# Requests for broadcast rows moved to later cycles, inverse rows made by exponentials, and a reordered last block

## The chip, the cores and the metric

The kernel runs on one core of a Trainium2 chip. The metric is the device time of one execution in microseconds (us). A core has five engines that each work through their own queue of instructions: TensorE (PE in the profile, its weight loads apart as PEld), VectorE (DVE), ScalarE (ACT), GpSimd (POOL) and SyncE (SP). SP and POOL ask for most of the transfers between the chip's main memory (DRAM) and the on-chip memory. Matrix products are written to PSUM[...].

## The reference

Two layers over 4096 nodes with 512 features, each followed by a residual and a layernorm. Layer 0 is graph attention with 8 heads of 64 features and a dense 0/1 adjacency of 4096 x 4096; its cost is the sums over all pairs of nodes.

```python
feats = jnp.einsum('nf,hfo->hno', X, W)
s_self = jnp.einsum('hno,ho->hn', feats, a_self)
s_neigh = jnp.einsum('hno,ho->hn', feats, a_neigh)
dense = s_self[:, :, None] + s_neigh[:, None, :]
dense = jnp.where(dense > 0, dense, ALPHA * dense)      # ALPHA = 0.2
dense = dense * A[None, :, :]
attn = jax.nn.softmax(dense, axis=-1)
out = jnp.einsum('hij,hjo->hio', attn, feats) + b[:, None, :]
...
x = _layernorm(x + relu(out of all heads side by side))
...
# layer 1: attention inside 32 graphs of 128 nodes, with query, key, value products,
# the adjacency added to the scores twice; then again residual and layernorm
```

## The kernel before, in words

The exponential of a leaky sum of two scores is the larger of two products of factors that belong to one node each, so a pair costs no exponential of its own. Setup computes for every node and head the factors exp(s), exp(0.2 s), exp(0.8 s) and exp(-0.2 s). For the receiving node (index i, along the free axis) they are needed as rows that are the same in all 128 partitions: row p = exp(0.8 s_i) and row u = exp(-0.2 s_i), and for some heads also U = 1/u. For the sending node (index j, along the partitions) they are columns: `d_all`, `e_all`, its bf16 parts `e_b`, and `c_all`, the reciprocal of one of them.

**Setup** runs over 8 blocks of four 128-node tiles. Per block: transposes of x, the feature products (L818), the scores, exponentials on ScalarE (L750, L751, L754), scaled features to DRAM (`f_d`, `g_d`), and the function `rows_of_exponentials`: two reciprocals (L780) on VectorE make U for the first and last pair of heads, four transposes (L786) turn the block's columns into 20 rows, ScalarE copies them (L793), POOL writes them to `pu_d` in DRAM. `parts_of_exponentials` makes `c_all` with two reciprocals per block (L762).

**The main part** is `main_pass(r)` for r = 0 to 3, one pair of heads each. A pass has 4 chunks (c) of 1024 receiving nodes, and a chunk goes over the 32 sending tiles j in cycles: eight tiles per cycle in passes 0 to 2, four in pass 3. For a tile j and each of the two heads

- VectorE makes q = max(p_row, d) times the adjacency tile (L1534),
- a mark of where the max took p_row is made by ScalarE (L1544) or, for every fourth tile's second head, by VectorE (L1539),
- TensorE adds q times g_s into `acc` (L1581), the adjacency tile times f_s into `accf` (L1558, four matmuls per tile), and the marks times e_b into `dens` (L1597).

A *folded* tile leaves out the L1558 products. VectorE makes its q with two operations instead of one (L1522 with the U row, L1525 with c_all), and TensorE adds q into `accf` instead of `acc`. In pass 0 the folded tiles are 10 and 18 in chunk 0 and 2, 10 and 18 in the others; in pass 3 a table gives them.

Within a cycle the order on TensorE is written out by hand: L1558 for all tiles of the cycle, transposes for the first half of the next cycle's adjacency (L617, pass 0 only), L1581 for all tiles, L1597, sums over the adjacency (L1479, pass 0), transposes for the other half. q has 8 buffers, so VectorE works up to four tiles ahead of L1581.

In pass 0 the adjacency arrives from DRAM as a_b: POOL asks for blocks of four tiles (L605, three buffers, each asked for ten tiles ahead at a fixed place of POOL's order), TensorE transposes them, ScalarE casts them to `at` (L628), and POOL writes each `at` tile to `at_d` for the later passes (L629). Passes 1 to 3 read `at_d`.

SP asks per chunk for the rows: p (two rows of 512 KB, L1434, two buffers each), u (two halves of 256 KB, L1440, one buffer), and U where tiles are folded (two of 512 KB, L1462, in the buffers `ck`); and per four tiles for f_s (512 KB, L1496) and g_s (256 KB, L1501), two buffers each. The p and u requests stand at the head of a chunk in the program; for chunks 0 and 1 of pass 0 they are kept in program order, otherwise a scheduler that plans all engines but TensorE may move them ahead as far as buffers allow.

At the end of a chunk VectorE combines the sums, (accf + S) * u_row (L1278), then adds acc (L1286); transposes and scaling follow in pieces during the next chunk.

**The last part** is layer 1, in 8 blocks of four 128-node rows; most of it runs between cycles of pass 3, the rest after it. For the last block `values(u)` makes a value product (L1186, four products of 512 columns, each two matmul records in the trace) and adds a bias on VectorE (L1194), and `rows_out` multiplies by the attention (L1200), adds the residual (L1202), and does the layernorm (L520, L521 on VectorE, L523, L524 on POOL, L528 on VectorE) and the output transfer. Before: values 2, values 3, then rows 2, rows 3.

Of the kernel before, what the change touches and what calls it, by code (L numbers as in the profile page):

```python
# [10 lines left out]
F32 = mybir.dt.float32  # L11
# [393 lines left out]
def adjacency_streamed_path(  # L405
# [58 lines left out]
    FOLDED = (0, PR - 1)  # L464
    FOLDS = {4: (1,), 5: (0, 1), 6: (0, 1, 2)}, {2: (1,), 4: (1,), 5: (0, 1), 6: (0, 1, 2)}
    HU = 2 * len(FOLDED)
    pu_d = dram.tile([2 * H + HU, N], F32, name="pu_d")
    at_d = dram.tile([NCH, NT, P, C], F32, name="at_d")
# [17 lines left out]
    for c in range(FC):  # L486
# [11 lines left out]
    nb_all = const.tile([P, NT, H], F32, name="nb_all")  # L498
    c_all = {
        r: (const if r else early).tile([P, NT, 2], F32, name="c_all") for r in FOLDED  # L500
    }
    below_0 = const.tile([P, 1], F32, name="below_0")
# [136 lines left out]
    with tc.tile_pool(name="setup1", bufs=1, side="right") as one, tc.tile_pool(  # L639
# [60 lines left out]
        for c in range(FC // 2):  # L700
            score_columns(c, False)
        powers = one.tile([P, 5, H], F32, name="powers")
        for i, v in enumerate((ALPHA, 1.0, ALPHA - 1.0, 1.0 - ALPHA, -ALPHA)):
            nc.vector.memset(powers[:, i, :], v)
# [32 lines left out]
        def exponentials(k, u, sc):  # L737

            j = 4 * k + u
            if u == 0:  # L740
                pu_js[k] = two.tile([P, 4, 2 * H + HU], F32, name="pu_j")
            st = small.tile([P, 5, H], F32, name="st")
            for lo, hi, w in ((0, 3, 1), (3, 5, 0)):
                ends_of_setup["DVE", u] = nc.vector.tensor_tensor(
                    st[:, lo:hi].rearrange("p k (q h) -> p k q h", q=2),
                    sc[:, None, :, :, w].to_broadcast([P, hi - lo, 2, H // 2]),
                    powers[:, lo:hi].rearrange("p k (q h) -> p k q h", q=2),
                    OP.mult,
                )
            nc.scalar.activation(e_all[:, j], st[:, 0:2], AF.Exp)  # L750
            nc.scalar.activation(  # L751
                pu_js[k][:, u, : 2 * H].rearrange("p (k h) -> p k h", k=2), st[:, 3:5], AF.Exp
            )
            nc.scalar.activation(d_all[:, j, :], st[:, 2], AF.Exp)  # L754

        def parts_of_exponentials(k):
            blk = slice(4 * k, 4 * k + 4)
            nc.vector.tensor_scalar_mul(
                nb_all[:, blk, :], d_all[:, blk, :], -BIG * (1.0 + 2.0**-23)
            )  # L760
            for r in FOLDED:
                nc.vector.reciprocal(  # L762
                    c_all[r][:, blk], e_all[:, blk, 1, 2 * r : 2 * r + 2]
                )
            eb = e_b[:, blk]
            for i in range(2):
                src = e_all[:, blk, i, :]
                rest = small.tile([P, 4, H], F32, name="rest")
                nc.vector.tensor_copy(eb[:, :, :, 3 * i], src)
                nc.vector.tensor_sub(rest, src, eb[:, :, :, 3 * i])  # L770
                nc.vector.tensor_copy(eb[:, :, :, 3 * i + 1], rest)
                nc.vector.tensor_sub(eb[:, :, :, 3 * i + 2], rest, eb[:, :, :, 3 * i + 1])
            nc.vector.tensor_copy(
                e_p[:, blk, :NE].rearrange("p j (m h) -> p j h m", h=H), eb[:, :, :, :3]
            )
            nc.vector.tensor_scalar_mul(eb[:, :, :, :3], eb[:, :, :, :3], -1.0)

        def rows_of_exponentials(k):
            for i, r in enumerate(FOLDED):
                nc.vector.reciprocal(  # L780
                    pu_js[k][:, :, 2 * H + 2 * i : 2 * H + 2 * i + 2],
                    pu_js[k][:, :, H + 2 * r : H + 2 * r + 2],
                )
            pr = pss.tile([2 * H + HU, 4, P], F32, name="ps_set")
            for u in range(4):
                nc.tensor.transpose(pr[:, u, :], pu_js[k][:, u], ident)  # L786
            if k < NB - 1:
                row = late.tile([2 * H + HU, 4 * P], F32, name="pu_row")
            else:
                row = hp_.tile([P, CT, FP], F32, name="hst")  # L790
                row = row.rearrange("p t n -> p (t n)")[: 2 * H + HU, : 4 * P]
            rows[k] = row
# [295 lines left out]
    def layer_1(blk, x1b, lp, lp1, lp2):  # L1088
# [93 lines left out]

        def values(u):
            pv = misc([P, F])
            for f in range(FC):
                nc.tensor.matmul(  # L1186
# [5 lines left out]
                )  # L1192
            vs[u] = lp.tile([P, F], F32, name="v_t")
            nc.vector.tensor_add(vs[u], pv, L1["bv"])  # L1194

# [26 lines left out]
        values(2)  # L1222
        values(3)
        yield
        if blk == NT // 4 - 1:
            rows_out((2,))
            rows_out((3,))
        else:
            rows_out((2, 3))
        yield  # L1230
# [193 lines left out]
    steps = [(r, c, j) for r in range(PR) for c in range(NCH) for j in range(NT)]  # L1424

    def main_pass(r, ae=None, wide=4):

        for c in range(NCH):
            p_row = []
            for h in range(2):  # L1430
                p_row.append(rowp.tile([P, C], F32, name=f"p_row{h}"))
                in_order(
                    r == 0 and c < 2,
                    nc.sync.dma_start(p_row[h], broadcast_rows(pu_d[2 * r + h, ts(c, C)], P, C)),  # L1434
                )
            u_row = urowp.tile([P, C], F32, name="u_row")
            for h in range(2):
                in_order(
                    r == 0 and c < 2,
                    nc.sync.dma_start(  # L1440
                        u_row[h * FH : (h + 1) * FH, :],
                        broadcast_rows(pu_d[H + 2 * r + h, ts(c, C)], FH, C),
                    ),
                )
            U_row = []

            def folded(j):

                if r == PR - 1:
                    return r in FOLDED and c > 0 and j % 4 in FOLDS[c > 1].get(j // 4, ())  # L1450
                return r in FOLDED and j % 8 == 2 and (0 if c else 8) < j < NT - 8

            def rows_for_folded():

                for h in range(2):
                    if r == PR - 1:
                        pool, shape, name = ((hp_, [P, CT, FP], "hst"), (pools.get("lp1"), [P, C], "U_row"))[h]
                    else:
# [4 lines left out]
                        U_row[h],  # L1463
                        broadcast_rows(pu_d[2 * H + 2 * FOLDED.index(r) + h, ts(c, C)], P, C),
                    )
# [24 lines left out]
            for j0 in range(0, NT, wide):  # L1490
# [3 lines left out]
                for k in range(j0 // 4, (j0 + wide) // 4):  # L1494
                    f_s[k] = fsp.tile([P, 4, 2, FP], F32R, name="f_s")
                    ins = nc.sync.dma_start(  # L1496
                        f_s[k].rearrange("p u s n -> p (u s n)").bitcast(F32), f_d[r, k]
                    )
# [4 lines left out]
                    )  # L1503
                    in_order(r == 0 and c == 0 and j0 < 16, ins)
                if at_step == 0:
                    cast_steps(0, 6, last_pair)
# [201 lines left out]
```

## Time and profile before

| | |
|---|---|
| median of 3 runs | 2042.51 us (2039.18 to 2042.93) |
| the profiled execution | 2043.19 us, span of its trace 2041.3 us |
| TensorE busy | 2005.9 us, 98% of the span |
| VectorE busy | 1744.8 us, 85% |
| ScalarE busy | 1533.1 us, 75% |
| mean transfer rate | 274 GB/s |
| q, L1534 (x962) | 1279 ns each |
| mark on ScalarE, L1544 (x834) | 1144 ns each |
| acc, L1581 (x7696) | 594 ns each, overlapping |
| accf, L1558 (x1924) | 400 ns each, overlapping |

The table's durations are those of single instructions. TensorE's matmuls overlap, so what counts there is the distance from one start to the next and the place where a stretch of them begins. "Span" is the time from the first to the last recorded instruction; the execution's own time is 1.9 us longer. The longer parts stand at: setup to about 160 us, pass 0 to about 560 us, passes 1 and 2 to about 1450 us, pass 3 and layer 1 to the end. A line of a timeline has the start, the duration, the engine, the line in the kernel, the operation, what is written and read, how many instructions are merged, and in brackets the idle time before it with what ended it. The SP lines are requests: the transfer itself lands some microseconds later.

### The profile page before, as it was taken

What the parts mean: (1) busy time and instruction counts of PE and PEld (TensorE: products, weight loads), DVE (VectorE), ACT (ScalarE), POOL (GpSimd) and SP (SyncE); (2) the same over time, 40 slices, a digit from 0 to 9 for tenths busy, and PEclk for the clock granted to TensorE, in tenths of its full rate; (3) what the DMA queues carried; (4) which work ended last, traced back from release to release, by engine and by line L of the source; (5) the groups of instructions that cost most, each with busy time, mean ns of one, the idle gap of its engine ahead of it and who ended that gap; (6) DMA issues with size and microseconds to landing.
All of it is one profiled execution on the core that took longest, in us unless ns stands there. A gap on an engine that the chain in (4) does not pass through costs nothing.

```text
span 2041.3 us, 38200 instructions
## 1 busy us (share of the span) xinstructions
PE 2005.9 (98%) x14981; PEld 1030.0 (50%) x14981; DVE 1744.8 (85%) x2219; ACT 1533.1 (75%) x1872; POOL 231.0 (11%) x362
## 2 busy tenths in 40 slices
PE   8999999999999999999999999999999999999997
PEld 7885545444444444444444544444444444445443
DVE  5668898898999998798999989999997897889754
ACT  3348988788888889788899889999786566567420
POOL 1222222222200000000000000000020210211111
PEclk9999999999999999999999999999999999999999
DMA  6899999999999999788999999989975775775211
GB/s 206 240 320 280 283 286 288 285 280 282 316 377 342 346 359 342 261 311 292 318 321 338 313 328 338 335 277 368 323 277 186 249 255 173 232 273 176 73 55 44
DMA packets 209386, 558.70 MB, mean 274 GB/s; under 512 B 25052, under 2 KB 66012, under 8 KB 209196
## 3 DMA queue, kind: packets, MB, share of 16 engines
q1 hardware_dynamic: 144844, 433.65, 61.0%
q0 software_dynamic: 62272, 121.98, 23.3%
q8 instruction: 120, 1.97, 0.4%
q10 hardware_dynamic: 2080, 0.52, 0.1%
q14 instruction: 70, 0.57, 0.1%
HBM read 499.13 MB, written 107.28 MB: 297 GB/s over the span
## 4 chain that ended last, share of the span: by engine, by line
PE 85%; DMA 7%; DVE 5%; issue 1%; ACT 1%; SPq 0%; POOL 0%; POOLq 0%; DVEq 0%; ACTq 0%
PE acc L1581 35%; PE accf L1558 20%; PE ps_fe L818 5%; PE ps_m L1186 5%; PE ps_m L1114 5%; PE dens L1597 5%; DMA a_b<-in_adj_dram 4%; DVE q L1534 3%; PE accf L1581 2%; PE ps_m L1141 1%; PE ps_m L1200 1%; DMA hp_l<-hs_d 1%; PE ps_m L617 1%; DMA at_d<-at 1%; PE ps_m L1043 1%
## 5 line engine op out<-in xcount | busy, mean ns | idle before, releaser
L1534 DVE SCALAR_TENSOR_TENSOR q<-p_row,d_all,at 128x1024 f32<-128x1024 f32 x962 | 1168.1, 1279 | 106.0 <-PE acc L1581 78.8
L1544 ACT ACTIVATE mark<-q,nb_all 128x1024 fp8e4<-128x1024 f32 x834 | 926.8, 1144 | 174.7 <-DVE q L1534 160.1
L1581 PE MATMUL acc<-q,g_s 128*32 128x512 f32 x7696 | 853.7, 594 | 1.1 <-DVE q L1534 0.4
L1581 PEld LDWEIGHTS acc<-q,g_s 128*32 128x32 f32 x7696 | 250.2, 110 | 557.2 <-issue 496.3
L1558 PE MATMUL accf<-at,f_s 128*128 128x512 f32 x1924 | 469.3, 400 | 1.7 <-ACT at L628 1.6
L1558 PEld LDWEIGHTS accf<-at,f_s 128*128 128x128 f32 x1924 | 357.2, 189 | 107.3 <-issue 27.8
L1249 ACT ACTIVATE ck<-ck,neg_half_f 128x1024 f32<-128x1024 f32 x128 | 146.0, 1141 | 28.5 <-DMA ck<-in_adj_dram 28.4
L1250 ACT ACTIVATE ck<-ck,neg_quarter 128x1024 f32<-128x1024 f32 x128 | 146.3, 1143 | 1.8
L1597 PE MATMUL dens<-mark,e_b 128*6 128x512 fp8e4 x2048 | 125.3, 379 | 2.5 <-DVE mark L1539 2.5
L818 PE MATMUL ps_fe<-w_sb_f,xT_f 128*128 128x264 f32 (+1 forms) x512 | 121.6, 395 | 1.7 <-ACT xT_f L730 1.7
L628 ACT CAST at<-ps_m 128x1024 fp32r<-128x1024 fp8e4 x124 | 116.3, 1022 | 4.8 <-issue 2.0
L1186 PE MATMUL ps_m<-wvT,x1T 128*128 128x512 f32 x256 | 114.2, 594 | 0.0
L1114 PE MATMUL ps_m<-x1T,M_sb 128*128 128x512 f32 x256 | 113.1, 595 | 0.0
L818 PEld LDWEIGHTS ps_fe<-w_sb_f,xT_f 128*128 128x128 f32 x512 | 100.5, 200 | 16.2 <-ACT xT_f L730 2.3
L1372 POOL DMA_DIRECT2D hs_d<-hst x12 | 10.7, 896 | 828.1 <-DVE hst L1362 817.5
L1539 DVE TENSOR_SCALAR mark<-q,d_all 128x1024 fp8e4<-128x1024 f32 x128 | 96.2, 751 | 4.7
L629 POOL DMA_DIRECT2D at_d<-at x128 | 69.1, 540 | 272.5 <-ACT at L628 94.0
L1597 PEld LDWEIGHTS <-e_b 128*6 128x6 bf16 x2048 | 55.9, 86 | 80.1 <-issue 38.2
L1529 ACT ACTIVATE mark<-q,below 128x1024 fp8e4<-128x1024 f32 x62 | 69.6, 1153 | 24.5 <-DVE q L1525 24.2
L1114 PEld LDWEIGHTS ps_m<-x1T,M_sb 128*128 128x128 f32 x256 | 48.0, 190 | 58.9 <-issue 57.1
L1525 DVE SCALAR_TENSOR_TENSOR q<-q,c_all,at 128x1024 f32<-128x1024 f32 x62 | 77.3, 1273 | 0.0
L1186 PEld LDWEIGHTS ps_m<-wvT,x1T 128*128 128x128 f32 x256 | 47.7, 190 | 56.3 <-issue 55.1
(207 smaller groups left out, 1294.9 us busy)
## 6 DMA issues: line engine op xcount, KB each, us to landing
at<-at_d SPq DMA_DIRECT2D x384, 512.0 KB, 6.1
f_s<-f_d SPq DMA_DIRECT2D x128, 512.0 KB, 7.8
at_d<-at POOLq DMA_DIRECT2D x128, 512.0 KB, 19.1
ck<-in_adj_dram SPq DMA_DIRECT2D x128, 512.0 KB, 5.5
g_s<-g_d SPq DMA_DIRECT2D x128, 256.0 KB, 5.9
f_d<-fst POOLq DMA_DIRECT2D x16, 1024.0 KB, 7.5
a_b<-in_adj_dram POOLq DMA_DIRECT2D x32, 512.0 KB, 21.7
p_row<-pu_d SPq DMA_DIRECT2D x32, 512.0 KB, 6.7
```

What stands on the lines that cost most here:

```text
L628: ends_of_setup["ACT"] = nc.scalar.copy(at, both[:, :, k])
L818: nc.tensor.matmul(pf[:, q, :, cols], tile_j(xTs[k][:, c].rearrange("p u n -> p (u n)"), u), w_sb[:, c, 4 * q : 4 * q + 4, cols], start=(c ...
L1114: nc.tensor.matmul(pz, L1["M"][:, f, ts(c, P)], x1T[:, f, :], start=(f == 0), stop=(f == FC - 1),)
L1186: nc.tensor.matmul(pv, x1T[:, f, ts(u, P)], L1["wvT"][:, f, :], start=(f == 0), stop=(f == FC - 1),)
L1249: tc.keep_in_program_order(nc.scalar.activation(ck, ck, AF.Square, bias=neg_half))
L1250: nc.scalar.activation(ck, ck, AF.Abs, bias=neg_quarter, accum_out=binp[:, k : k + 1])
L1534: ends_of_setup["Q"] = nc.vector.scalar_tensor_tensor(q, p_row[h], d_j, ats[r, c, j].bitcast(F32), op0=OP.max, op1=OP.mult)
L1539: nc.vector.tensor_scalar(mark, q, d_j, None, op0=OP.is_gt, saturate=False)
L1544: nc.scalar.activation(mark, q, AF.Sigmoid, bias=nb_all[:, j, hh : hh + 1], scale=BIG, saturate=False,)
L1558: nc.tensor.matmul(accf[:, s, :], f_s[j // 4][:, j % 4, w, :], ats[r, c, j][:, ts(s, HB)], start=(j == 0 and w == 0), stop=(j == NT - 1 an ...
L1581: nc.tensor.matmul(dst[o : o + 32, s, :], g_s[j // 4][:, j % 4, h, o % FH : o % FH + 32], qs[j, h][:, ts(s, HB)], start=(j == 0), stop=(j ...
L1597: nc.tensor.matmul(dens[lo : lo + 6, :], e_b[:, j, 2 * r + h, :], marks[j, h][:, ts(s, HB)], start=(j == 0), stop=(j == NT - 1),)
```

## The change

1. All four pairs get a U row: `powers` has a sixth entry (exp(0.2 s)), the activation L751 writes three rows of eight heads instead of two, L786 transposes 24 columns instead of 20, `pu_d` has 24 rows. The reciprocals at L780 go.
2. `c_all` for the last pass is no longer made per block in setup; at the start of that pass it is summed from the parts in `e_b` and inverted.
3. In pass 0 the folded tiles are 8, 16 and 24 of every chunk (three in chunk 0 instead of two).
4. f_s is loaded only from the first to the last tile of a group that isn't folded.
5. In pass 0 the requests for u of chunks 1 to 3 stand at tile 8 of their own chunk, and those for p of the next chunk at tile 16, all kept in program order. Other passes as before.
6. In the last block, row block 2 is finished between the third and the fourth product of values 3.

```diff
-    FOLDS = {4: (1,), 5: (0, 1), 6: (0, 1, 2)}, {2: (1,), 4: (1,), 5: (0, 1), 6: (0, 1, 2)}
-    HU = 2 * len(FOLDED)
-    pu_d = dram.tile([2 * H + HU, N], F32, name="pu_d")
+    FOLDS = {1: {4: (1,), 5: (0, 1), 6: (0, 1, 2)}, 2: {2: (1,), 4: (1,), 5: (0, 1), 6: (0, 1, 2)}, 3: {2: (1,), 4: (1,), 5: (0, 1), 6: (0, 1, 2)}}
+    pu_d = dram.tile([3 * H, N], F32, name="pu_d")
...
-        for i, v in enumerate((ALPHA, 1.0, ALPHA - 1.0, 1.0 - ALPHA, -ALPHA)):
+        for i, v in enumerate((ALPHA, 1.0, ALPHA - 1.0, 1.0 - ALPHA, -ALPHA, ALPHA)):
...
-            nc.scalar.activation(
-                pu_js[k][:, u, : 2 * H].rearrange("p (k h) -> p k h", k=2), st[:, 3:5], AF.Exp
-            )
+            nc.scalar.activation(pu_js[k][:, u], st[:, 3:6], AF.Exp)
...
-            for r in FOLDED:
-                nc.vector.reciprocal(
-                    c_all[r][:, blk], e_all[:, blk, 1, 2 * r : 2 * r + 2]
-                )
+            nc.vector.reciprocal(c_all[0][:, blk], e_all[:, blk, 1, :2])
...
         def rows_of_exponentials(k):
-            for i, r in enumerate(FOLDED):
-                nc.vector.reciprocal(
-                    pu_js[k][:, :, 2 * H + 2 * i : 2 * H + 2 * i + 2],
-                    pu_js[k][:, :, H + 2 * r : H + 2 * r + 2],
-                )
...
-        def values(u):
-            pv = misc([P, F])
-            for f in range(FC):
+        def values(u, split=FC, pv=None):
+            if pv is None:
+                pv, fs = misc([P, F]), range(split)
+            else:
+                fs = range(split, FC)
+            for f in fs:
...
-            vs[u] = lp.tile([P, F], F32, name="v_t")
-            nc.vector.tensor_add(vs[u], pv, L1["bv"])
+            if fs[-1] == FC - 1:
+                vs[u] = lp.tile([P, F], F32, name="v_t")
+                nc.vector.tensor_add(vs[u], pv, L1["bv"])
+            return pv
...
         values(2)
-        values(3)
-        yield
         if blk == NT // 4 - 1:
+            last = values(3, 3)
             rows_out((2,))
+            values(3, 3, last)
+            yield
             rows_out((3,))
         else:
+            values(3)
+            yield
             rows_out((2, 3))
...
+    def load_p_rows(r, c, pinned):
+
+        rows = []
+        for h in range(2):
+            rows.append(rowp.tile([P, C], F32, name=f"p_row{h}"))
+            ins = nc.sync.dma_start(rows[h], broadcast_rows(pu_d[2 * r + h, ts(c, C)], P, C))
+            in_order(pinned, ins)
+        return rows
+
+    def load_u_row(r, c, pinned):
+
+        u_row = urowp.tile([P, C], F32, name="u_row")
+        for h in range(2):
+            ins = nc.sync.dma_start(
+                u_row[h * FH : (h + 1) * FH, :],
+                broadcast_rows(pu_d[H + 2 * r + h, ts(c, C)], FH, C),
+            )
+            in_order(pinned, ins)
+        return u_row
...
+        if r in FOLDED and r:
+            c_all[r] = c_r = pools["lp1" if r == PR - 1 else "wl1"].tile(
+                [P, NT, 2], F32, name="c_all"
+            )
+            e_r = e_b[:, :, 2 * r : 2 * r + 2, 3:]
+            nc.vector.tensor_tensor(c_r, e_r[:, :, :, 0], e_r[:, :, :, 1], OP.add)
+            nc.vector.tensor_tensor(c_r, c_r, e_r[:, :, :, 2], OP.add)
+            nc.vector.reciprocal(c_r, c_r)
         for c in range(NCH):
...
+            p_row = p_rows.pop((r, c), None) or load_p_rows(r, c, (r, c) == (0, 0))
+            if r or c == 0:
+                u_row = load_u_row(r, c, r == 0)
...
-                return r in FOLDED and j % 8 == 2 and (0 if c else 8) < j < NT - 8
+                return r in FOLDED and j % 8 == 0 and j > 0
...
-                        broadcast_rows(pu_d[2 * H + 2 * FOLDED.index(r) + h, ts(c, C)], P, C),
+                        broadcast_rows(pu_d[2 * H + 2 * r + h, ts(c, C)], P, C),
...
+                    live = [u for u in range(4) if not folded(4 * k + u)]
                     ins = nc.sync.dma_start(
-                        f_s[k].rearrange("p u s n -> p (u s n)").bitcast(F32), f_d[r, k]
+                        f_s[k][:, live[0] : live[-1] + 1].rearrange("p u s n -> p (u s n)").bitcast(F32),
+                        f_d[r, k, :, live[0] * 2 * FP : (live[-1] + 1) * 2 * FP],
                     )
...
+                if r == 0 and c and j0 == 8:
+                    u_row = load_u_row(r, c, True)
+                if r == 0 and c < NCH - 1 and j0 == 16:
+                    p_rows[r, c + 1] = load_p_rows(r, c + 1, True)
```

More of the change, by code (lines that the diff above doesn't have):

```diff
@@ L498, in adjacency_streamed_path @@
     nb_all = const.tile([P, NT, H], F32, name="nb_all")
-    c_all = {
-        r: (const if r else early).tile([P, NT, 2], F32, name="c_all") for r in FOLDED
-    }
+    c_all = {0: early.tile([P, NT, 2], F32, name="c_all")}
     below_0 = const.tile([P, 1], F32, name="below_0")
@@ L701, in adjacency_streamed_path @@
             score_columns(c, False)
-        powers = one.tile([P, 5, H], F32, name="powers")
-        for i, v in enumerate((ALPHA, 1.0, ALPHA - 1.0, 1.0 - ALPHA, -ALPHA)):
+        powers = one.tile([P, 6, H], F32, name="powers")
+        for i, v in enumerate((ALPHA, 1.0, ALPHA - 1.0, 1.0 - ALPHA, -ALPHA, ALPHA)):
             nc.vector.memset(powers[:, i, :], v)
@@ L740, in exponentials @@
             if u == 0:
-                pu_js[k] = two.tile([P, 4, 2 * H + HU], F32, name="pu_j")
-            st = small.tile([P, 5, H], F32, name="st")
-            for lo, hi, w in ((0, 3, 1), (3, 5, 0)):
+                pu_js[k] = two.tile([P, 4, 3, H], F32, name="pu_j")
+            st = small.tile([P, 6, H], F32, name="st")
+            for lo, hi, w in ((0, 3, 1), (3, 6, 0)):
                 ends_of_setup["DVE", u] = nc.vector.tensor_tensor(
@@ L778, in rows_of_exponentials @@
         def rows_of_exponentials(k):
-            for i, r in enumerate(FOLDED):
-                nc.vector.reciprocal(
-                    pu_js[k][:, :, 2 * H + 2 * i : 2 * H + 2 * i + 2],
-                    pu_js[k][:, :, H + 2 * r : H + 2 * r + 2],
-                )
-            pr = pss.tile([2 * H + HU, 4, P], F32, name="ps_set")
-            for u in range(4):
-                nc.tensor.transpose(pr[:, u, :], pu_js[k][:, u], ident)
+            pr = pss.tile([3 * H, 4, P], F32, name="ps_set")
+            for u in range(4):
+                nc.tensor.transpose(
+                    pr[:, u, :], pu_js[k][:, u].rearrange("p k h -> p (k h)"), ident
+                )
             if k < NB - 1:
-                row = late.tile([2 * H + HU, 4 * P], F32, name="pu_row")
+                row = late.tile([3 * H, 4 * P], F32, name="pu_row")
             else:
                 row = hp_.tile([P, CT, FP], F32, name="hst")
-                row = row.rearrange("p t n -> p (t n)")[: 2 * H + HU, : 4 * P]
+                row = row.rearrange("p t n -> p (t n)")[: 3 * H, : 4 * P]
             rows[k] = row
@@ L1424, in adjacency_streamed_path @@
     steps = [(r, c, j) for r in range(PR) for c in range(NCH) for j in range(NT)]
-    def main_pass(r, ae=None, wide=4):
-        for c in range(NCH):
[L1429 to L1434, printed above, removed]
-                )
[L1436 to L1444, printed above, removed]
+    p_rows = {}
+    def load_p_rows(r, c, pinned):
[14 more added lines that the diff above has]
+        return u_row
+    def main_pass(r, ae=None, wide=4):
+        if r in FOLDED and r:
[6 more added lines that the diff above has]
+            nc.vector.reciprocal(c_r, c_r)
+        for c in range(NCH):
+            p_row = p_rows.pop((r, c), None) or load_p_rows(r, c, (r, c) == (0, 0))
+            if r or c == 0:
+                u_row = load_u_row(r, c, r == 0)
             U_row = []
@@ L1449, in folded @@
                 if r == PR - 1:
-                    return r in FOLDED and c > 0 and j % 4 in FOLDS[c > 1].get(j // 4, ())
-                return r in FOLDED and j % 8 == 2 and (0 if c else 8) < j < NT - 8
+                    return r in FOLDED and c > 0 and j % 4 in FOLDS[c].get(j // 4, ())
+                return r in FOLDED and j % 8 == 0 and j > 0
             def rows_for_folded():
```

## The prediction

> **What bounds the kernel now.** I read the page first: the engine shares, the slices, the chain. TensorE is busy in 98% of the span and nearly all of the chain lies on it, so an edit pays only where TensorE stands still, runs slowly or does less. The second line below is the busy share of the DMA engines: all through the first pass (slices 4 to 11, some 155 to 560 us) it is full as well, so in this pass a late transfer can stop TensorE.
>
> ```profile
> PE   8999999999999999999999999999999999999997
> DMA  6899999999999999788999999989975775775211
> ```
>
> Next the waits of TensorE in that pass (us in total, times, longest): three times the transposes L617 wait for adjacency blocks that POOL asks for.
>
> ```profile
> PE ps_m L617 <- DMA a_b<-in_adj_dram: 6.2, 3, 3.6
> ```
>
> The timeline of TensorE gives the places: 0.41 us before 272.24, 3.63 before 379.89, 2.19 before 487.78. Each is the first cycle of a chunk (c = 1, 2, 3), where the block for tiles 8 to 11 is needed. The worst one:
>
> ```profile
> 369.24 7.01 PE L1558 MATMUL accf<-at,f_s 128*128 128x512 f32 x28
> 379.89 1.07 PE L617 MATMUL ps_m<-ident_b,a_b 128*128 128x128 bf16 x16 [3.63 <-DMA a_b<-in_adj_dram]
> 380.88 5.31 PE L1581 MATMUL acc<-q,g_s 128*32 128x512 f32 x32
> ```
>
> Those 32 matmuls take 3.64 us elsewhere (273.23, 488.78), so 1.7 us more is lost to a slow clock. What SP had asked for just before, and how long the block travelled in the chain (start, duration):
>
> ```profile
> 318.02 1.60 SPq L1462 DMA_DIRECT2D ck<-pu_d  x2
> ...
> 347.38 4.00 SPq L1496 DMA_DIRECT2D f_s<-f_d  x2
> 352.38 1.09 SPq L1440 DMA_DIRECT2D u_row<-pu_d  x2
> ...
> 362.38 1.51 SPq L1434 DMA_DIRECT2D p_row<-pu_d  x2
> ```
> ```profile
> 352.91 26.93 DMA a_b<-in_adj_dram
> ```
>
> The reader is to see that the u and p rows fall into the 27 us in which the block is under way; the median for such a block is 21.7 us. The three late ones took 28.0, 26.9 and 26.5.
>
> The same timeline shows two waits of setup and a slow start:
>
> ```profile
> 43.77 0.60 PE L786 MATMUL ps_set<-ident_f,pu_j 128*20 128x128 f32 x4 [1.22 <-DVE pu_j L780]
> ...
> 157.94 0.60 PE L786 MATMUL ps_set<-ident_f,pu_j 128*20 128x128 f32 x4 [1.22 <-DVE pu_j L780]
> 160.17 10.20 PE L1558 MATMUL accf<-at,f_s 128*128 128x512 f32 x32 [1.63 <-ACT at L628]
> ```
>
> Thirty-two such matmuls take 7.56 us at 239.08. The table of stretches (PEclk, DMA share and GB/s are the last three) has the reason:
>
> ```profile
> 160.00:166.00 6.00, 5.83 (x14) 4.59 (x15) 5.70 (x6) 5.97 (x7) 4.97 (x8) 0.51 0.76 258
> ...
> 381.00:384.00 3.00, 3.00 (x16) 0.68 (x20) 0.00 (x0) 2.74 (x4) 0.54 (x1) 0.50 1.03 419
> ```
>
> And VectorE at the end:
>
> ```profile
> 2026.72 0.69 DVE L1194 TENSOR_TENSOR v_t<-ps_m,bv_row 128x512 f32<-128x512 f32 x1 [2.09 <-PE ps_m L1186]
> 2027.58 0.75 DVE L1202 SCALAR_TENSOR_TENSOR y_f<-ps_m,rd_f,x1b 128x512 f32<-128x512 f32 x1 [0.17 <-PE ps_m L1200]
> 2028.37 0.69 DVE L520 BATCH_NORM_STATS2 stats_f<-y_f 128x6 f32<-128x512 f32 x1
> 2028.98 0.73 DVE L1202 SCALAR_TENSOR_TENSOR y_f<-ps_m,rd_f,x1b 128x512 f32<-128x512 f32 x1
> ```
>
> **What the Trainium skill says.** "DMA: Bandwidth & Descriptors", section "Issuing engines are not separate DMA queues": transfers started by SP, ACT and POOL run on the same 16 engines and interleave. The trace agrees: SP's rows lengthen POOL's block by 5 us. "TensorE: Matmul & The Clock Gate", section "What's actually happening": the array runs at half clock until it has been busy for a window of about 3.4 us, falls back after an idle one, and the windows run freely. The trace agrees: 0.50 follows the wait of 3.63 us; after the one of 2.19 us the clock was 1.00. The same page, "Architectural detail", calls the queues of ScalarE and VectorE strict FIFO, so an operation that waits holds up what stands behind it; I use that for the tail.
>
> **The change part by part.**
>
> *Reciprocals to exponentials.* The two reciprocals per block at L780 go (0.2 us each, VectorE); the activation L751 writes 24 columns where it wrote 16 (0.20 us, at most 0.05 more, ScalarE idle beside it). A block's last exponential is done well before L786 at 43.77 (32.4 us), so that wait of 1.22 us goes. TensorE has no gap from there to 156.7, so the gain is kept: **-1.2**. At 157.94, L786 would start at some 156.8, after L751 (156.48 to 156.69). The ROW copy L793 then no longer stands behind two casts: the built order of ScalarE has one cast (ends 157.8), the copy (0.5), the cast of tile 5 (1.0), which L1558 waits for: 159.25 instead of 160.17, **-0.9**. The half-clock spell (159 to 165.8) cost 12 matmuls at 0.43 instead of 0.23, 2.4 us. The thin stretch before it shrinks from 5.0 us (155.2 to 160.2) to 4.0, still over a window, so I keep the spell. If it goes, TensorE gains up to 2.2 more, no further, since VectorE ends its first eight q at 170.1 as now (169.7). Ends: 0 and -3.1.
>
> *One fold more.* Folded tiles are 8, 16, 24 in every chunk; chunk 0 had two, now three. A folded tile spares the first-pass product four matmuls: 7.56 us against 6.69 (214.17), **-0.9**. VectorE has 2 x 1.2 us more in that cycle; it waits 1.5 to 1.9 us per cycle for q buffers, and a cycle of 25 us with a fold already holds 23 us of its work, so it is hidden; if that cover failed it would cost up to 1 us. For the other chunks the folds only move. L1278 now has to wait for tile 24's products as well; it stands behind eight q, where VectorE had a ninth, so it delays nothing.
>
> *The rows.* At the 285 GB/s of these slices 1 MB takes 3.7 us. u and p (0.5 + 1 MB, 5.5 us) leave the stretch between 347 and 380: u is asked for at tile 8 (about 397), p of the next chunk at tile 16 (about 315, in the place that U has now). But U (1 MB) waits for a buffer that tile 24's fold frees instead of tile 18's: its two DMAs go from 318 to some 340, shortly before the block. That puts 3.7 us back, less what drains in the 10 to 15 us between; I take 2.2. Two f_s loads in the stretch lose 128 KB each: 0.9. Sum for chunk 2: -5.5 + 2.2 - 0.9 = -4.2, more than the wait of 3.63, which goes with its clock loss of 1.7. Chunk 1 likewise: 0.41 goes. In chunk 3, p of the second pass is not pinned and stays in the built order where it is now (472): -1.8 (u) + 2.2 - 0.9 = -0.5; and the queue no longer has chunk 2's 5.3 us of standstill to catch up in, for which I add 0.7: 2.2 becomes 2.4. Waits of 7.9 become 2.4: **-5.5**. Ends: all gone, -7.9; lateness only pushed into chunk 3, where 4.6 and a cold 1.7 stand, -1.6. SP itself waits nowhere longer: the new u and p requests stand behind g_s loads that already wait 7 us, with f_s behind them needed a cycle later.
>
> *c_all of the last pass.* Two small additions and a reciprocal on VectorE, some 0.4 us by the rows of L770 and L762 (0.15 and 0.13 for half the elements), go to the start of the last pass, where VectorE is the later one (L1581 at 1467.02 takes 9.46 us for what takes 7.07): **+0.4**, ends 0 and 0.6. One reciprocal per block (0.13) leaves setup, hidden. The shorter f_s loads of the last pass hide too: nothing waits for f_s there.
>
> *Tail.* Row block 2's product goes ahead of the last value product. TensorE's end of block 3's values moves by two matmuls (0.86), from 2026.7 to 2027.6. VectorE's order becomes y2, its statistics, then the bias add of 3: 2028.1 to 2028.8. Product 3 is ready 1.2 us later as now, 2029.95; but the scaling of y2 (0.5) comes ahead of y3 and waits for POOL, so y3 starts at 2030.4 instead of 2028.98. The rest (0.65 + 0.65 + 0.15 + 0.9 POOL + 0.5) ends at 2033.4 instead of 2033.0: **+0.4**, ends -0.5 (POOL faster) and +0.6.
>
> Sum: -1.2 - 0.9 - 0.9 - 5.5 + 0.4 + 0.4 = -7.7. The profiled execution took 2043.2 (span 2041.3), 0.7 above the median of 2042.5; so 2035.5 in its terms and 2034.8 against the median. I give 2035.
>
> **Rivals.** (B) The first pass is bound by DMA throughput, so lateness moves rather than goes. For: a DMA share above 1.0 in every stretch. Against: within a chunk the blocks regain up to 10 us. Then the waits give -1.6: 2042.5 - 3.8 = 2038.7. (C) All waits and the half-clock spell go: -1.2 - 3.1 - 0.9 - 7.9 + 0.4 = -12.7, 2030. For: the blocks then have 4 us of margin. Against: p of the second pass. (D) Slower: U's later request, with p 25 us ahead of it, makes blocks later than now. It decides from the point where U's 3.7 us do not drain at all before tile 8: waits of 2, 3.6 and 8 us with two cold windows, 17 against 7.9, give -3.0 + 0.8 + 9.1 = +6.9, 2049. Against: u and p together are more than U.
>
> **Numbers.** Forecast 0.50, B 0.26, C 0.19, D 0.05. A measurement of this kernel can tell about 0.2%, 4.1 us, from no change. Below 2038.4 lie C, nine tenths of the forecast and a little of B: 0.68; the rest of B and of the forecast 0.27; D 0.05. The range 2030 to 2041 takes in C's value, B and the worse ends of single terms.
>
> **What would show it.** L786 without waits at 43 and 157; L1558 at about 158 (1.2 earlier for setup); accf x28 in the last cycle of chunk 0; no wait for a_b at tile 8 of chunks 1 and 2, one of 2 to 3 us in chunk 3; U's DMAs asked for after tile 24's fold; y3's scaling 5.3 us after the last value product ends (5.8 now). Waits as long as now in chunks 2 and 3 would make it wrong.

## The result, and the profile after

| | before | after |
|---|---|---|
| median beside each other | 2042.61 us (2037.71 to 2045.53) | 2032.36 us (2031.17 to 2032.90) |
| ratio, 95% interval | | 0.9955 (0.9944 to 0.9965) |
| profiled execution, span | 2043.19, 2041.3 us | 2031.95, 2030.0 us |
| TensorE busy | 2005.9 us | 2001.7 us |

A second measurement of the same pair gave 2039.69 and 2033.08 us, ratio 0.9971 (0.9959 to 0.9982). By these ratios the change is worth 6 to 9 us. The executions of the kernel before spread more than that: over all that were made beside the experiments they run from 2033.7 to 2045.5, and the profiled one, 2043.19, lies in the upper part. A ratio of kernels measured beside each other says more here than a difference of two medians, and since the same pair gave 0.9955 and 0.9971, ratios of different sets of runs can differ by 0.0016 without any edit.

The page's slices of the kernel after: TensorE's row is now full from the first slice on, and the transfers (second row) are as busy as they were.

```profile
PE   9999999999999999999999999999999999999997
DMA  6999999999999999898999899989976775775211
```

The waits of TensorE in the first pass (line, what for; us in total, times, longest). The line for a_b, 6.2 us before, is not there any more. The chain of work that ended last, which held three blocks of 26 to 28 us before, holds none now. There is one wait that was not there before, for VectorE's copy L794.

```profile
PE accf L1578 <- ACT at L625: 2.7, 4, 2.1
PE ps_m L614 <- DVE pu_all L794: 1.8, 1, 1.8
PE ps_m L614 <- DVE hst L1309: 1.1, 3, 0.4
```

TensorE's timeline at the first cycle of chunk 2, where it stood 3.63 us: the transposes L614 follow the products at once, and the granted clock was 1.00 there.

```profile
365.31 7.60 PE L1578 MATMUL accf<-at,f_s 128*128 128x512 f32 x32
372.75 1.07 PE L614 MATMUL ps_m<-ident_b,a_b 128*128 128x128 bf16 x16
373.75 6.64 PE L1601 MATMUL acc<-q,g_s 128*32 128x512 f32 x60
```

The rows of SP's timeline for the same stretch, and then the block's own request with the time to its landing. p of chunk 2 is asked for at 310, U at 334 and 337 (318 before), u not before 388. The block travels 21.0 us, before 26.9.

```profile
310.11 1.43 SPq L1430 DMA_DIRECT2D p_row<-pu_d  x2
...
334.31 0.32 SPq L1476 DMA_DIRECT2D ck<-pu_d  x1
337.36 0.32 SPq L1476 DMA_DIRECT2D ck<-pu_d  x1
...
388.12 1.15 SPq L1438 DMA_DIRECT2D u_row<-pu_d  x2
```
```profile
L602 POOL DMA_DIRECT2D a_b<-in_adj_dram x1: 896/896/896, 347.3 to 347.3; - x1
...
DMA to landing us min/median/max: 21.0/21.0/21.0
```

Setup and the start of the first pass on TensorE. L773 (L786 before) starts without a wait both times; the products L1578 start at 155.97 instead of 160.17. But at 167.71 TensorE stands 1.76 us.

```profile
40.47 0.60 PE L773 MATMUL ps_set<-ident_f,pu_j 128*24 128x128 f32 x4
...
153.28 0.60 PE L773 MATMUL ps_set<-ident_f,pu_j 128*24 128x128 f32 x4
155.97 9.08 PE L1578 MATMUL accf<-at,f_s 128*128 128x512 f32 x32 [2.10 <-ACT at L625]
...
167.71 0.61 PE L614 MATMUL ps_m<-ident_b,a_b 128*128 128x128 bf16 x8 [1.76 <-DVE pu_all L794]
```

The two stretches at that place (PEclk, DMA share and GB/s last): half clock now lasts one window of 3.4 us, up to 159.2, and not two.

```profile
156.00:160.00 4.00, 4.00 (x11) 3.22 (x12) 3.90 (x5) 3.97 (x5) 3.79 (x5) 0.60 0.76 273
160.00:166.00 6.00, 5.95 (x35) 4.63 (x34) 6.00 (x6) 5.77 (x6) 1.15 (x3) 1.00 1.05 221
```

VectorE explains the new wait. The copy that gives the PSUM buffer back stands behind eight q and a mark. Before, VectorE was through with these at 170.5 and waited for TensorE; now TensorE is earlier by more than VectorE is.

```profile
157.09 9.65 DVE L1554 SCALAR_TENSOR_TENSOR q<-p_row,d_all,at 128x1024 f32<-128x1024 f32 x8
166.77 0.75 DVE L1559 TENSOR_SCALAR mark<-q,d_all 128x1024 fp8e4<-128x1024 f32 x1
167.44 0.22 DVE L794 COPY pu_all<-ps_m 128x64 f32<-128x64 f32 x1
```

At the end of the program, VectorE: y2 is scaled at 2018.50, ahead of y3's addition, as the built order had it.

```profile
2016.73 0.67 DVE L1187 TENSOR_TENSOR v_t<-ps_m,bv_row 128x512 f32<-128x512 f32 x1
...
2018.50 0.55 DVE L525 TENSOR_SCALAR y_f<-y_f,mv_f,rstd_f 128x512 f32<-128x512 f32 x1 [1.01 <-POOL rstd_f L521]
2018.96 0.74 DVE L1196 SCALAR_TENSOR_TENSOR y_f<-ps_m,rd_f,x1b 128x512 f32<-128x512 f32 x1
```

Where the 11.3 us between the two profiled spans lie, taken from the starts of the same instruction in both traces (for pass 0, the first mark product of each cycle):

| stretch | after less before, us |
|---|---|
| setup up to the first L773 | -3.3: the wait -1.2, one window of half clock less -1.75, first loads -0.35 |
| from there to the first L1578 | -0.9 |
| first cycle | +0.8: one window of half clock less -1.1, the wait for the copy +1.8, rest +0.1 |
| rest of chunk 0; chunk 1; chunk 2; chunk 3 | -0.2; -0.3; -5.3; -2.1 |
| first six cycles of pass 1 | +1.4: f_s late once 0.8, VectorE late from chunk 3's last fold 0.6 |
| start of pass 3; rest of pass 3 and layer 1 | +0.5; -1.4 |
| from there to the last scaling; last output | 0.0 (the tail +0.6, a shorter wait for x1b -0.6); -0.5 |

### The profile page after: what moved, and what is told of

Same layout as the page of the kernel before. It is cut to its first block, busy times and chain, and to the rows that moved or that the text cites. A ratio compares the mean times of both kernels' runs of the same rounds, so it can differ in the third digit from the quotient of the medians.

```text
span 2030.0 us, 38112 instructions
## 1 busy us (share of the span) xinstructions
PE 2001.7 (99%) x14977; PEld 1025.7 (51%) x14977; DVE 1746.5 (86%) x2201; ACT 1524.4 (75%) x1872; POOL 232.8 (11%) x362
## 3 DMA queue, kind: packets, MB, share of 16 engines
q0 software_dynamic: 62272, 122.04, 23.3%
## 4 chain that ended last, share of the span: by engine, by line
PE 83%; DVE 9%; issue 2%; DMA 2%; ACT 2%; SPq 0%; POOL 0%; DVEq 0%; POOLq 0%; ACTq 0%
PE acc L1601 34%; PE accf L1578 20%; PE ps_fe L807 5%; PE ps_m L1178 5%; DVE q L1554 5%; PE ps_m L1103 5%; PE dens L1617 4%; PE accf L1601 2%; PE ps_m L1130 1%; PE ps_m L1194 1%; DVE q L1542 1%; DVE q L1545 1%; ACT at L625 1%; PE ps_m L614 1%; PE ps_m L1083 1%
## 5 line engine op out<-in xcount | busy, mean ns | idle before, releaser
L1564 ACT ACTIVATE mark<-q,nb_all 128x1024 fp8e4<-128x1024 f32 x832 | 916.7, 1149 | 140.1 <-DVE q L1554 128.3
L1578 PE MATMUL accf<-at,f_s 128*128 128x512 f32 x1920 | 467.9, 399 | 3.7 <-ACT at L625 2.7
L1578 PEld LDWEIGHTS accf<-at,f_s 128*128 128x128 f32 x1920 | 354.2, 188 | 110.8 <-issue 26.5
L1246 ACT ACTIVATE ck<-ck,neg_half_f 128x1024 f32<-128x1024 f32 x128 | 146.0, 1140 | 25.7 <-DMA ck<-in_adj_dram 25.7
```

Source lines behind the costliest of these rows:

```text
L1246: tc.keep_in_program_order(nc.scalar.activation(ck, ck, AF.Square, bias=neg_half))
L1564: nc.scalar.activation(mark, q, AF.Sigmoid, bias=nb_all[:, j, hh : hh + 1], scale=BIG, saturate=False,)
L1578: nc.tensor.matmul(accf[:, s, :], f_s[j // 4][:, j % 4, w, :], ats[r, c, j][:, ts(s, HB)], start=(j == 0 and w == 0), stop=(j == NT - 1 an ...
```

## The experiments

Each experiment was measured several times beside the kernel before on one chip; the ratio is to those runs. Four sets were measured, each on its own chip: rows, exponentials, folds and the changed kernel without the rows; the changed kernel again, whole f_s, old tail and early copy; POOL's order, folds and rows, early copy with old tail; p of the second pass. Two theories stood at first. R: the u and p rows in flight beside a block make it late, so part 5 alone removes the waits. T (called B later, as in the prediction): the transfers of pass 0 are one full queue, so moving requests only moves lateness.

**The rows alone.** `load_p_rows` and `load_u_row` with their two calls, and nothing else of the change.

```diff
+                if r == 0 and c and j0 == 8:
+                    u_row = load_u_row(r, c, True)
+                if r == 0 and c < NCH - 1 and j0 == 16:
+                    p_rows[r, c + 1] = load_p_rows(r, c + 1, True)
```

> The kernel before with part 5 alone: u of chunks 1 to 3 asked for at tile 8 of its own chunk, p of the next chunk at tile 16; folds, tail and setup as before. Theory R (the rows in flight beside the block make it late): no wait for a_b at tile 8 in chunks 1 and 2, at most 1 us in chunk 3, no half-clock spell at 380: 7 to 8 us less than before. Theory T (the whole queue is behind, and what helped in the changed kernel was the shorter f_s loads, U's later place and the 3 us that setup ends earlier): waits of 4 us or more stay, under 4 us gained.

Measured: ratio 0.9999 (0.9991 to 1.0007), no gain. The block of tile 8 in chunk 2 did travel only 19.8 us. But p and U were now asked for together, 2 MB within 6 us (before, p stood apart at 362):

```profile
311.88 1.75 SPq L1433 DMA_DIRECT2D p_row<-pu_d  x2
316.18 1.60 SPq L1471 DMA_DIRECT2D ck<-pu_d  x2
```

The block asked for at 307.4 took 28.9 us (its like before 23.7), the next one 27.6 (22.9), and in chunk 2, where p and U were again asked for together at 415.7 and 420.0, TensorE waited at a place where it had not waited, for tile 24:

```profile
427.86 1.07 PE L617 MATMUL ps_m<-ident_b,a_b 128*128 128x128 bf16 x16 [1.77 <-DMA a_b<-in_adj_dram]
```

R falls as it was put: with the rows moved the travel of the block for tile 8 is shorter by 7.1 us in chunk 2 and 3.4 in chunk 3, but moving them in this manner made other blocks late. In this profile the waits for a_b are 2.7 us in all where they were 6.2; it is of the fastest of the 14 executions (2034.95, median 2037.00), so the ratio and not the profile tells what the edit is worth.

**Exponentials alone** (parts 1 and 2; the rest as before).

> The kernel before with parts 1 and 2 alone: rows of exp(0.2 s) from the exponentials, c_all of the last pass summed at its start. Setup loses the 1.22 us before L773 and starts pass 0 about 0.9 sooner; c_all costs 0.45. If the half-clock spells are shorter because of the missing wait, 3.0 us less than before; if their length is chance, 1.7 less. Theory R: the three waits for a_b stay as they are (POOL asks 3 us sooner as well). Theory T: they shrink by up to 3 us in all, 5 us less than before.

Measured: ratio 0.9993 (0.9985 to 1.0001), some 1.4 us, with an interval that includes no gain at all. In its profile L773 has no wait and the products start 2.4 us sooner; the waits for a_b were 2.4 and 1.0, each 1.2 us shorter than before. The time is about the 1.7 us that was expected without shorter waits, and far from the 5 of theory T. The profile has two windows of half clock in setup, as before, so the window that setup lost in the kernel after isn't from the missing wait.

**Folds and shorter f_s alone.**

```diff
-                return r in FOLDED and j % 8 == 2 and (0 if c else 8) < j < NT - 8
+                return r in FOLDED and j % 8 == 0 and j > 0
...
+                    live = [u for u in range(4) if not folded(4 * k + u)]
```

> The kernel before with parts 3 and 4 alone: folded tiles 8, 16, 24 in every chunk, f_s loaded only from the first to the last tile that is not folded. Theory R: the waits for a_b stay within 2 us of what they are (6.2 in all), the extra fold gives 0.3 to 0.9: within 2 us of before. Theory T: less to load and U out of the way, waits fall under 3 us, 3 to 5 us less. Rival D of the prediction (U's later request collides with the block): waits grow, up to 7 us more than before.

Measured: ratio 0.9988 (0.9981 to 0.9995), 2.4 us. The waits for a_b were 1.1 and 0.15, less than R expects, while the time falls short of the 3 to 5 us of T.

```profile
PE ps_m L617 <- DMA a_b<-in_adj_dram: 1.2, 2, 1.1
```

Rival D's collision doesn't occur. The block of tile 8 in chunk 2 still travelled 27.0 us, but was asked for 25.9 us before its use and not 23.3.

**The changed kernel without the rows.**

```diff
-            p_row = p_rows.pop((r, c), None) or load_p_rows(r, c, (r, c) == (0, 0))
-            if r or c == 0:
-                u_row = load_u_row(r, c, r == 0)
+            p_row = load_p_rows(r, c, r == 0 and c < 2)
+            u_row = load_u_row(r, c, r == 0 and c < 2)
```

> The changed kernel with part 5 undone: u and p asked for at the head of a chunk as before. Theory R: waits for a_b of 5 us or more in all come back, with or without a half-clock spell: 5 to 8 us more than the changed kernel (2037 to 2040). Theory T: at most 2 us more than the changed kernel.

Measured: ratio 0.9973 (0.9965 to 0.9980), and no wait for a_b at all in its profile. The block travelled 25.7 us, and was asked for 27.4 us ahead:

```profile
L602 POOL DMA_DIRECT2D a_b<-in_adj_dram x1: 898/898/898, 345.6 to 345.6; - x1
...
DMA to landing us min/median/max: 25.7/25.7/25.7
```

In the same set the rows alone, the exponentials alone and the folds alone had 0.9999, 0.9993 and 0.9988. So most of the gain comes without the part that the change is named after. To compare, the changed kernel was measured again, together with three relatives.

> The changed kernel as it is, beside the three below. Theory B (the transfers of pass 0 are one queue that is full; taking bytes out is what helps, moving requests about is not): the ratio to before is that of the kernel without part 5 (0.9973) within 0.001. Theory M (several moves are needed together, part 5 among them, for the margins at tile 8): 0.9955 again, 0.0015 or more below it.

Measured: ratio 0.9971 (0.9959 to 0.9982), that of the kernel without the rows, as B expects and not M. Against the first measurement, 0.9955, the rows could still be worth up to 0.0018, since the kernel without them was not measured in one set with the changed kernel. But neither kernel's profile, with the rows or without, has a wait for a_b left.

**Whole f_s loads.** Part 4 undone (`live` and the slice go).

> The changed kernel with part 4 undone: f_s whole (512 KB) also for the groups that start with a folded tile, 3 x 128 KB more per chunk. Theory B: at 285 GB/s that is 1.35 us per chunk, so by the end of chunk 3 blocks are 4 to 5 us later than in the changed kernel, where the least margin was 1.0: waits of 3 to 4 us for a_b in chunks 2 and 3 and perhaps a half-clock spell, 3 to 5 us more than the changed kernel. Theory M: at most 1 us more.

Measured: ratio 0.9968 (0.9959 to 0.9978), no loss. The added bytes show where they should, but less than expected: the margin at tile 8 of chunk 3 fell from 1.0 and 1.5 (two profiles of the changed kernel) to a wait of 0.2, and doesn't add up over chunks, since blocks regain time within each.

```profile
PE ps_m L614 <- DMA a_b<-in_adj_dram: 0.2, 1, 0.2
```

That counts against B in its plain form: 0.39 MB more per chunk in a full queue did not lengthen the time.

**The old tail.** Part 6 undone.

```diff
-            last = values(3, 3)
-            rows_out((2,))
-            values(3, 3, last)
+            values(3)
             yield
+            rows_out((2,))
             rows_out((3,))
```

> The changed kernel with part 6 undone: values 3 whole, then row blocks 2 and 3. In the profiles the tail from the first residual addition of row block 1 to the last scaling took 0.6 us more with the change, and the output transfers 0.5 less. If that 0.5 belongs to the order (the last two outputs no longer close together) the time stays within 0.3 us; if it is chance, 0.6 us less than the changed kernel.

Measured: ratio 0.9968 (0.9956 to 0.9980) against 0.9971. Between the two profiles the stretch from pass 3's last marks to the last scaling is 0.6 us shorter with the old order, and the output transfers differ by 0.2; the times can't tell 0.6 us.

**The early copy.** L791 and L794 ahead of the first cycle's products. The result of L791 goes to a PSUM buffer of setup (`ps_set`) as well, where the changed kernel takes one of those (`ps_m`) that L614 uses next.

```diff
+        columns_of_exponentials(NB - 1)
         for j in (12, 16):
...
-        columns_of_exponentials(NB - 1, misc([P, 4, 2 * H]))
...
-                if at_step == 0:
-                    columns_of_last()
```

> The changed kernel with the last block's transposes L791 and VectorE's copy L794 put ahead of the first cycle's products, where TensorE waits for ScalarE's cast anyway; in the changed kernel the copy stood behind eight q and TensorE waited 1.76 us for it at 167.7. If that wait is lost time: 1.3 to 1.8 us less than the changed kernel, no wait of L614 in the first cycle. If VectorE's q are the real bound of that cycle: the same time, a wait of L1601 or of a later cycle in its place.

Measured: ratio 0.9945 (0.9931 to 0.9958), the fastest of all: 2028.82 us beside 2033.08 for the changed kernel. TensorE does L791 in a stretch where it stands for ScalarE anyway (the products start 2.7 us after L773 as in the changed kernel), and L614 goes through:

```profile
155.35 0.42 PE L791 MATMUL ps_set<-ident_f,hst 16*128 16x16 f32 x4 [1.20 <-ACT hst L782]
156.25 9.10 PE L1575 MATMUL accf<-at,f_s 128*128 128x512 f32 x32 [0.48 <-ACT at L625]
165.19 1.07 PE L614 MATMUL ps_m<-ident_b,a_b 128*128 128x128 bf16 x16
```

At the first mark products TensorE is 2.1 us ahead of the changed kernel beside it (179.9 for 182.1). Order and buffer changed together, so which of the two removed the wait is not shown. A wait of 1.3 for a_b came back at tile 8 of chunk 3, where the block was asked for 22.6 us before its use and not 25.2, and at the end of pass 2 only 0.5 us of the lead is left. The gain of 4.3 between the medians is more than the 1.3 to 1.8 that was expected: most of it lies in pass 3 and layer 1, where the profile of the changed kernel beside it has 1.5 us more at the start and a window of half clock more. Nothing shows that the early copy causes this.

**POOL's order.** A theory L: the block is late because POOL asks late, standing 5.3 us for the rows `hs_d` first.

```diff
-                nc.gpsimd.dma_start(
+                (nc.gpsimd if r else nc.sync).dma_start(
                     hs_d[ts(c, C), ts(r, FP)].rearrange("(t p) n -> p t n", p=P), hst
```

> The kernel before, with one edit: in pass 0 the finished rows hs_d (1 MB per chunk, L1372) are written by a request of SP instead of POOL. In the kernel before POOL stood 5.3 us for this request at 348.5, with adjacency writes and the request for the block of tile 8 (352.9) behind it. Theory L (the block is late because POOL asks late): it is asked for 3 to 5 us sooner, the waits of TensorE for a_b in chunks 2 and 3 fall below 1 us each, 3 to 5 us less than before. Theory B (the transfers of pass 0 are one full queue): POOL's other transfers wait for one another as before, the waits stay within 2 us in sum, the time within 1.5 us.

Measured: ratio 1.0000 (0.9991 to 1.0008). POOL stands as long for something else, a landing block, and the block for tile 8 took 30.1 us:

```profile
347.53 0.53 POOL L629 DMA_DIRECT2D at_d<-at  x1 [6.06 <-DMA a_b<-in_adj_dram]
...
350.50 0.90 POOL L605 DMA_DIRECT2D a_b<-in_adj_dram  x1 [0.95 <-PE ps_m L617]
```
```profile
380.65 1.89 PE L617 MATMUL ps_m<-ident_b,a_b 128*128 128x128 bf16 x16 [6.18 <-DMA a_b<-in_adj_dram]
```

L falls for chunk 2: the block was asked for only 0.6 us further ahead of its use than before, and POOL waited for its own earlier transfers instead. In chunk 3 it was asked for 26.6 us ahead (24.3 before), travelled 24.2, and TensorE did not wait; so the waits moved into one, and their sum stayed 6.2 us, as B has it.

**Folds and rows together**, without parts 1, 2, 4 and 6.

> The kernel before with parts 3 and 5 alone: folded tiles 8, 16, 24, u at tile 8, p of the next chunk at tile 16; f_s whole, setup and tail as before. Theory I (the two work together: later folds move U away from the p request, and the rows leave the block's flight): no wait for a_b in any chunk, margins of 3 us and more at tile 8 of chunk 2, 4 us or more less than before (ratio 0.998 or lower). Theory S (the sooner end of setup is what makes the margin): waits of 1 us or more stay, ratio about that of folds alone (0.9988).

Measured: ratio 0.9973 (0.9958 to 0.9988), where in another set the rows alone gave 0.9999 and the folds with the shorter f_s 0.9988. In its profile, that of the slowest of the six executions (2040.75, the fastest 2033.15), chunks 1 and 2 have no wait and margins of 4.9 and 3.5 us at tile 8; chunk 3 has one of 2.4, and then a window of half clock.

```profile
481.35 1.82 PE L617 MATMUL ps_m<-ident_b,a_b 128*128 128x128 bf16 x16 [2.41 <-DMA a_b<-in_adj_dram]
```

Theory I holds in chunks 1 and 2 and not in chunk 3. The ratio leans to I, but its interval reaches the 0.9988 of theory S. In chunk 3 the changed kernel, which has the sooner setup and the shorter f_s besides, does not wait.

**The early copy with the old tail.**

> The changed kernel with the early copy (L794 ahead of the first cycle) and the old order of the last block. If the two add up as their profiles say: 0.4 to 0.6 us less than with the early copy alone, ratio to before 0.994; a wait for a_b of about 1 us at tile 8 of chunk 3 stays.

Measured: ratio 0.9941 (0.9928 to 0.9955), against 0.9945 for the early copy alone: the tail's 0.6 us stays below what can be told. In its profile a_b is nowhere waited for, with 0.4 us to spare at tile 8 of chunk 3.

**p of the second pass.** On top of the early copy.

```diff
-                if r == 0 and c < NCH - 1 and j0 == 16:
-                    p_rows[r, c + 1] = load_p_rows(r, c + 1, True)
+                if r == 0 and j0 == 16:
+                    nxt = (0, c + 1) if c < NCH - 1 else (1, 0)
+                    p_rows[nxt] = load_p_rows(*nxt, True)
```

> The changed kernel with the early copy, and p of pass 1 asked for at tile 16 of chunk 3 of pass 0, kept in program order (in the changed kernel it is asked for at 462.5, while the block for tile 8 of chunk 3 is under way from 452.3 to 475.8). If these rows are why that block has the least margin of all (1.0 us in the changed kernel, a wait of 1.3 with the early copy alone): it lands in about 21 us instead of 23.9, margin 2 us or more at tile 8 of chunk 3, no wait, 1 us less than with the early copy alone (ratio to before about 0.994). If lateness only moves on: another block of chunk 3 (tiles 16 or 24), or p at the start of pass 1, is waited for, and the time is that of the early copy.

Measured: ratio 0.9960 (0.9946 to 0.9973). The block does what was expected, 20.4 us instead of 23.9, and TensorE has 4.0 us to spare where it waited 1.3; no other block is late.

```profile
L602 POOL DMA_DIRECT2D a_b<-in_adj_dram x1: 896/896/896, 449.5 to 449.5; - x1
...
DMA to landing us min/median/max: 20.4/20.4/20.4
```

A gain of about 1 us over the early copy is not seen: the two intervals overlap, and they are from different chips. Whether these rows cost something elsewhere stays open.

The block for tile 8 in the profiles that bear on it: its lead, which is how long before its use it was asked for (the wait taken off), less its travel from the request to the landing, and what is left as margin, in us. The margin was rounded after the subtraction; where it is negative, TensorE waited.

| kernel | chunk 2 | chunk 3 |
|---|---|---|
| before | 23.3 - 26.9 = -3.6 | 24.3 - 26.5 = -2.2 |
| rows alone | 21.6 - 19.8 = 1.9 | 22.3 - 23.1 = -0.8 |
| exponentials alone | 24.6 - 27.0 = -2.4 | 25.7 - 26.7 = -1.0 |
| folds and f_s alone | 25.9 - 27.0 = -1.1 | 25.3 - 25.4 = -0.1 |
| folds and rows | 24.7 - 21.2 = 3.5 | 22.3 - 24.7 = -2.4 |
| changed, without rows | 27.4 - 25.7 = 1.7 | 26.5 - 25.7 = 0.8 |
| changed | 25.4 - 21.0 = 4.4 | 24.5 - 23.4 = 1.0 |
| changed, whole f_s | 25.6 - 21.4 = 4.2 | 23.0 - 23.1 = -0.2 |
| POOL's order | 24.0 - 30.1 = -6.1 | 26.6 - 24.2 = 2.4 |
| early copy | 24.0 - 20.3 = 3.7 | 22.6 - 23.9 = -1.3 |
| early copy, p of pass 1 | 25.3 - 21.0 = 4.3 | 24.4 - 20.4 = 4.0 |

Moving the rows shortens the travel (the second number of a column): by 4.7 to 7.1 us in chunk 2 and 0.7 to 3.4 in chunk 3. It also costs lead (the first number), 2.0 us between the changed kernel without the rows and with them. The other parts add lead: the folds with the shorter f_s 2.6 us in chunk 2 and 1.0 in chunk 3, the exponentials alone 1.3 and 1.4. In chunk 2 the rows by themselves leave no wait at tile 8, and so does everything else without the rows, which is why taking the rows out brings no wait back. The changed kernel without its folds was not run, so what the folds are worth in it stays open. That later folds let POOL ask sooner because U's megabyte leaves the time in which the blocks before are under way fits the margins at tile 0 of chunk 2 (2.9 us before, 5.8 with folds and f_s alone), but this was not tried by itself.

## Why the prediction was right, and where not

It gave 2035 against 2032.36, within its range; its sum was -7.7, the two measurements of the pair -9 and -6 by their ratios. That TensorE stood for late blocks, and that these waits would go, was right. That the total came so near is in part luck: the path by which the waits go was not the one of the sum, as the rows below show, and two things at the start of pass 0 that the sum didn't hold nearly cancel: a window of half clock that went (1.1 us gained) and the wait for the copy (1.8 lost). By its steps:

- **L786, -1.2**: as predicted; all kernels with part 1 have no wait there, all without have it.
- **Start of pass 0, -0.9**: as predicted. But "so I keep the spell" did not hold: half of the spell went. The five profiles without part 1 have two windows of half clock there, the nine with it one. That gave 1.1, and the step behind it was missed: not the q but the copy L794, queued behind them, sets when TensorE goes on, 1.8 us lost. The early copy shows that this was real time in the first cycle (2.1 us).
- **One fold more, -0.9**: the wrong size. The cycle with tile 24 gained 0.5 (25.26 for 25.78), but chunk 0 as a whole 0.2. That the fold is hidden does not hold at the end of the pass: with tile 24 folded in the last cycle VectorE comes 0.6 late into pass 1, in every kernel with part 3 and in none without.
- **The rows, -5.5**: the term furthest off. The waits of 7.9 (6.2 and the clock's 1.7) went whole, as in rival C, where 2.4 had been left in chunk 3. The 5.5 us for u and p in chunk 2 was near: the travel is 5.9 shorter. But U's later request was booked as a cost of 2.2, and no such cost appears: with the folds and the shorter f_s alone the travel stayed (27.0 for 26.9, 25.4 for 26.5), the lead grew, and the waits fell from 6.2 to 1.2. The shorter f_s was put at 0.9 (1.2 to 1.7 in chunk 3) and the sooner setup at nothing (with the exponentials alone each of the two waits is 1.2 shorter). So moving the rows, by far the largest item of the sum, was not needed to end the waits, and what the sum took for a cost, for 0.9 or for nothing was enough without it (25.7 us of travel, and no wait). That folds and rows without the rest also wait 2.4 in chunk 3 is a likeness of numbers only, from the slowest of six executions.
- **What the sum was made against**: the profiled execution stood 7.9 us and took 2043.19, but others of the same kernel took down to 2033.7. There is one profile of this kernel, so where the faster executions save their time is not shown. By the ratios the same change was worth 9 us at one time and 6 at another.
- **c_all, +0.4**: not clear. The three operations took 1.0 us (0.26, 0.22 and 0.54 from 1346.9 on) where 0.4 was put, and the place was misread: in the kernel before, pass 0 ends at 583 us and pass 3 begins at 1355.47, not at about 560 and 1450, and the products at 1467.02 belong to chunk 1 of pass 3 and not to its start. The first chunk of pass 3 took 0 to 1.5 us longer in kernels with part 2, and 1.0 and 1.2 longer in two without.
- **Tail, +0.4**: 0.6 in the profiles, at the upper end of its bounds, below what times can tell.
- **Rivals**: B is half right. Lateness moved on when the rows alone were moved, but 0.39 MB per chunk more did not make the kernel slower. D's collision isn't there: with U later and the rows where they were, waits were shorter than before.

## What to carry to other kernels

A transfer is late by two numbers, when it is asked for and how long it travels; edits that act on one and on the other need not add up, and an edit that looks decisive may not be needed once another has made room. When a wait is taken from one engine, look for the next thing that the same engine needs from a busier one, even a copy of 0.2 us: its place in the other's queue can be the new bound. Before a wait seen in one profile is booked as a gain, look at how far the executions of the kernel spread.

## What the runs showed that I had not expected

- Half clock came in windows of 3.41 us or two of them. In setup the profiles had two, one or none without regard to the edits. In layer 1 (before L1083 of the changed kernel, at 1954 to 1970 us) TensorE waits 1.6 to 2.5 us in all 14 profiles; five of them had a window of half clock there, after waits of 2.0 to 2.2 us, and six others none after waits of 2.1 to 2.5. A window at half speed costs 1.7 us. After the 6.18 in chunk 2 there were two. The Trainium skill, "TensorE: Matmul & The Clock Gate", section "What's actually happening", says that the windows run freely and that the clock falls after an idle one of about 3.4 us. The first agrees with these profiles (in the kernel before, the starts of half clock lie 38 and 65 windows of 3.413 us apart); for the second, waits of 2.0 us were enough here. So a single profile can be 2 us from its like for no reason in the kernel.
- Moving a 1 MB write from POOL's requests to SP's, with POOL's 5.3 us wait gone, changed nothing (1.0000): POOL then stood 6.06 us for a block, and the block behind it travelled 30.1 us.
